# W_out's slabs turned on VectorE in 32 x 32 squares instead of on TensorE, with norm_w applied to the attention heads

## The chip, the cores and the metric

The kernel runs on one core of a Trainium2 chip (trn2). The metric is the device time of the whole launch in microseconds, the median of three runs. All data are float32.

## The reference, cut to what matters

The whole computation is a block of five stages on x of shape (4, 512, 512): a recurrent mix (bi-directional WKV), a gated-delta attention with 16 query heads and 32 value heads, a residual, a second WKV mix and a binarised linear layer. The change touches only the end of the attention: each value head's output h is normalised, multiplied by `norm_w` (one weight for each of the 128 head dimensions) and by silu(z), and then projected with `W_out`.

```python
h = core.astype(jnp.float32)                     # (4, 512, 32, 128)
h = h * jax.lax.rsqrt(jnp.mean(h * h, axis=-1, keepdims=True) + EPS)
h = norm_w * h * jax.nn.silu(z.astype(jnp.float32))
out = jnp.einsum('bsf,df->bsd', h.reshape(Bq, Sq, HV * HD), W_out)   # W_out: (512, 4096)
...
x = x + _L0_attn_ref(...)
```

For one value head the projection is a product of h (512 tokens x 128) with the transpose of a slab of `W_out`, 512 x 128. TensorE contracts over the partitions, so it needs the slab with its 128 head dimensions f on the partitions and the 512 outputs d along the row. In memory `W_out` has d as rows: the slab must be turned.

## The kernel before, in words

**Units and steps.** The attention's work is cut into 64 units, numbered n = b * 16 + hq: batch b (0 to 3) and query head hq (0 to 15); a unit has two value heads, h = 0 and 1. The loop at the end of the kernel (line 1706) makes 66 steps. A step i works on several units at once, each at a different stage: unit i + 6 (K in the plan, keys), i (F, projections and queries), i - 1 (C, the chunks of the recurrence), i - 2 (O, the output's norm, W_out's slab) and i - 3 (W, the output product). The table `plan` (line 1173) lists, for each of 22 slots of a step, what is issued in which order; slots count from 0. Every instruction goes through `InOrder` (line 72), so each engine executes exactly in this written order. SP issues almost all DMAs, in the same order, and a DMA that waits for its buffer or its data holds all later DMAs on SP.

**W_out's slab in batch 0.** Only the first batch reads W_out itself. `out_start(n, h)` (line 451) loads the 512 x 128 slab of head h in slots 13 (h = 0) and 15 (h = 1), with d on the partitions, as four blocks of 128, into a buffer of the pool `ld` with tag "raw" (four buffers of 2 KB per partition, shared with all other slab loads). `out_turn(n, h)` (line 471) turns it with four TensorE transposes into one PSUM bank, in slots 18 and 19. `out_end` (line 478) copies the bank to SBUF on ScalarE and multiplies by norm_w (`nw`, one scalar per partition) on the way: for h = 0 in two halves, the right half into a "raw" buffer of its own, `b12`; for h = 1 in one piece. The tile `wo` has seven slots of 256 columns. `out_forms` (line 492, slot 20) makes the four sums T1 to T4 of a Strassen-Winograd product from the four quarters B11, B12, B21, B22; `spare` puts it on VectorE for every fourth unit and on GpSimd otherwise. T3 and T4, T1, T2 take the other slots of `wo`. Last, SP stores `wo` and `b12` in the DRAM scratch `wosc`.

**The other batches** load `wo` from `wosc` in slot 13. The very last unit has a plain product and loads B11, B12 (index 7 of `wosc`), B21 and B22.

**The head's side.** `head_turn` (line 989) turns the normalised head output on TensorE, `head_end` (line 995, slots 7 and 10) copies the bank to `hS` on ScalarE with a plain copy, `head_forms` makes four sums, and `out_product` (line 1013) multiplies seven times. The results are added to x by VectorE in `out_add`.

**Neighbours that matter.** In batch 0 the slabs of W_qkvz are turned in the same way: `slab_start` loads, `slab_turn` transposes on TensorE, `slab_end` (line 426) copies on ScalarE, after which `project` (line 505) uses the slab. The slab of K goes through slots 3, 4 and 5, that of F's last value head through slots 9, 10 and 11. `gap_load(F + 1, "t")` in slot 21 loads the tile `dkt` for the next step; GpSimd masks it (slot 1) and ScalarE exponentiates it in slots 3 and 4, ahead of the slab copy of slot 4. `queries_end` (slot 21) multiplies dkt on VectorE with ps_kq. `inverse_load` (slot 16), `gap_load(K + 1, "d")` (slot 18) and `key_blocks` (slot 19) are SP's other DMAs around the change. `wkv_over` (slots 18, 19) holds the half reciprocals that some steps have on VectorE.

The profile has one line number for nearly everything, line 80, the helper through which all instructions pass. Groups are therefore told by tile: ps_wo is the bank of W_out's turn, woraw its load, b is b12, wo the seven slots, w a slab of W_qkvz, ps_p the bank of `project`.

Of the kernel before, what the change touches and what calls it, by code (L numbers as in the profile page):

```python
# [9 lines left out]
F32 = mybir.dt.float32  # L10
I32 = mybir.dt.int32
AF = mybir.ActivationFunctionType
ALU = mybir.AluOpType
# [3 lines left out]
P = 128  # L17
# [23 lines left out]
def kernel(  # L41
# [21 lines left out]
    B, S, D = x.shape  # L63
    HV = A_log.shape[0]
    HQ = HV // 2
    HD = norm_w.shape[0]
    KT = D // P
# [15 lines left out]
    V, A, G, T, Q = (InOrder(e) for e in (nc.vector, nc.scalar, nc.gpsimd, nc.tensor, nc.sync))  # L83
    NB = P // BS
    NM = 2 * NC
    NU = B * HQ
# [6 lines left out]
    def bank(tag, name):  # L93
        return pp.tile([P, 512], F32, tag=tag, name=name, bufs=banks[tag])


    ident = const.tile([P, P], F32, name="ident")
# [7 lines left out]
        out=tri_le, in_=tri_le, compare_op=ALU.is_ge, fill=0.0, base=0,  # L105
# [5 lines left out]
        out=tri_gt, in_=tri_gt, compare_op=ALU.is_gt, fill=0.0, base=0,  # L111
# [8 lines left out]
    for i in range(3):  # L120
        t = const.tile([P, NM, P], F32, name=f"inv_t{i}")
        G.memset(t, 0.0)
        inv_t.append(t)
        t = const.tile([P, NM // 2, 3 * BS], F32, name=f"inv_n{i}")
# [7 lines left out]
    nw = const.tile([P, 1], F32, name="nw")  # L132
# [6 lines left out]
    wosc = dram.tile([HQ, P, 8, D // 2], F32, name="wosc")  # L139
# [6 lines left out]
    with ExitStack() as main:  # L146
# [4 lines left out]
        ld = main.enter_context(tc.tile_pool(name="ld", bufs=4))  # L151
# [12 lines left out]
        def unit(n):  # L164

            return (*divmod(n, HQ), units.setdefault(n, {}))
# [32 lines left out]
        scale = const.tile([P, B], F32, name="scale")  # L199
# [240 lines left out]
        SB = {"B11": 0, "B21": 1, "B22": 2, "T1": 3, "T2": 4, "T3": 5, "T4": 6}  # L440
# [4 lines left out]
        D2 = D // 2  # L445

        def spare(i):

            return V if i % GROUP == 2 else G

        def out_start(n, h):

            b, hq, u = unit(n)
            if n == NU - 1:
                w = u[f"wo{h}"] = wp.tile([P, D], F32, **WO_LAST[h], name=f"wo_{n}_{h}")
                for i, at in enumerate(((0, 7), (1, 2))[h]):
                    Q.dma_start(out=w[:, i * D2 : (i + 1) * D2], in_=wosc[hq, :, at])
                return
            if h == 0:
                u["wo"] = wp.tile([P, 7, D2], F32, tag="wo", name=f"wo_{n}")  # L460
                if b:
                    Q.dma_start(out=u["wo"], in_=wosc[hq, :, :7])
            if b == 0:
                raw = u[f"woraw{h}"] = ld.tile([P, KT, P], F32, tag="raw", name=f"woraw_{n}_{h}")
                f = (2 * hq + h) * HD
                Q.dma_start(out=raw, in_=W_out[:, f : f + HD].rearrange("(n p) f -> p n f", p=P))


        WO_LAST = ({"tag": "wk", "bufs": 1}, {"tag": "wx", "bufs": 3})

        def out_turn(n, h):
            b, hq, u = unit(n)
            if b == 0:
                ps = u[f"wops{h}"] = bank("pj", f"ps_wo_{n}_{h}")
                for k in range(KT):
                    T.transpose(ps[:, k * P : (k + 1) * P], u[f"woraw{h}"][:, k, :], ident)

        def out_end(n, h):
            b, hq, u = unit(n)
            if b:  # L480
                return
            w, ps = u["wo"], u[f"wops{h}"]
            if h == 0:
                u["b12"] = ld.tile([P, D2], F32, tag="raw", name=f"b12_{n}")
                A.activation(w[:, 0], ps[:, :D2], AF.Copy, scale=nw)
                A.activation(u["b12"], ps[:, D2:], AF.Copy, scale=nw)
            else:
                A.activation(
                    w[:, 1:3].rearrange("p i d -> p (i d)"), ps, AF.Copy, scale=nw
                )  # L490

        def out_forms(n):
            b, hq, u = unit(n)
            if b:
                return
            w, b12, E = u["wo"], u["b12"], spare(n + 2)
            for out_, x_, y_ in (("T1", b12, "B11"), ("T2", "B22", "T1"), ("T3", "B22", b12), ("T4", "B21", "T2")):
                x_, y_ = (w[:, SB[v]] if isinstance(v, str) else v for v in (x_, y_))
                E.tensor_tensor(w[:, SB[out_]], x_, y_, ALU.subtract)
            if B > 1:  # L500
                Q.dma_start(out=wosc[hq, :, :7], in_=w)
                Q.dma_start(out=wosc[hq, :, 7], in_=b12)


        def project(n, r, half, tag="pp"):
# [489 lines left out]
        def head_end(n, h):  # L995
            b, hq, u = unit(n)
            if h == 0:
                u["hS"] = u1p.tile([P, 7, S // 2], F32, tag="hT", name=f"hS_{n}")

            at = u["hS"][:, 0:4:3] if h == 0 else u["hS"][:, 1:3]  # L1000
            A.copy(at, u["ps_h"].rearrange("p (t s) -> p t s", t=2))

        def head_forms(n):
            if n == NU - 1:
# [159 lines left out]
        def last_add(b, c):  # L1164
# [7 lines left out]
        K, F, C, O, W = AHEAD, 0, -1, -2, -3  # L1172
# [60 lines left out]
             (turn_end, F, 3), (square, F, 0), (key_matrix, K, 1), ("wkv", wkv_over, 0),  # L1233
             (gap_load, K + 1, "d"), (slab_start, K + 1, 1), ("sub", 17, None)],

            [(z_product, C, 1, 0), (out_turn, O, 1), (out_end, O, 0), (key_blocks, K), ("wkv", wkv_over, 1), ("gate", gates_rows), ("sub", 18, None)],

            [(chunk_t, C, 3), (norms, F, 0), (queries, F), (z_silu, C, 0), (out_end, O, 1),
             (out_forms, O), ("wkv", wkv_end), ("sub", 19, None)],

            [(z_product, C, 1, 1), (chunk_t_end, C, 3), (norms_copy, F, 0), (queries_end, F, 0), (queries_end, F, 1),
# [528 lines left out]
```

## Time and profile before

| | |
|---|---|
| median of three runs | 3054.6 us (3053.82 to 3056.66) |
| the profiled execution | 3053.92 us, its span 3052.2 us |
| mean granted TensorE clock | 0.985 |
| W_out's turn on TensorE | 128 matmuls of 128x128, 239.9 to 945.6 us |
| W_out's copies on ScalarE | 16 of 128x512, 32 of 128x256; 473 to 689 ns each |
| copies of the heads, hS<-ps_h | 128 of 128x512, 581 ns each |
| loads of W_out, woraw | 32 DMAs of 256 KB, 3.3 us to landing |
| stores wosc<-wo, wosc<-b | 16 of 896 KB, 3.7 us; 16 of 128 KB, 4.4 us |
| DMA packets | 422465, 351.75 MB, mean 115 GB/s |

How to read it: TensorE has two rows, PE for matmuls and transposes and PEld for the loading of the stationary operand, which overlaps. DVE is VectorE, ACT ScalarE, POOL GpSimd, SP the queue that issues DMAs. Batch 0's share of the span is about 240 to 960 us; one step takes some 44 to 49 us there.

### The profile page before, as it was taken

Reading aid. Unit: us, or ns where it says so; the run is one execution under the profiler, and the core shown is the slowest. Engines: PE = TensorE matmul, PEld = TensorE weight load, DVE = VectorE, ACT = ScalarE, POOL = GpSimd, SP = SyncE. Lnnn points to the kernel's source line nnn. Section 1 sums busy time; section 2 is a strip of 40 time slices with the busy share of each in tenths; the row PEclk is TensorE's granted clock in tenths of the full one; section 3 lists DMA queues with packets and bytes.
Section 4 is the critical chain, followed back from the end, with each engine's and each line's share of the span. In section 5 each row is a group of like instructions: output and inputs, shape, how many; then the busy total and the mean of one; then the engine's idle time right before and its main releaser. Section 6 shows DMA issues by size and latency. Waiting matters only on the chain.

```text
span 3052.2 us, 60274 instructions
## 1 busy us (share of the span) xinstructions
PE 2945.0 (96%) x20816; PEld 2124.5 (70%) x20816; DVE 2285.3 (75%) x5101; ACT 1881.6 (62%) x5145; POOL 1475.2 (48%) x3249
## 2 busy tenths in 40 slices
PE   7679999999999999999999999999999999999998
PEld 4447677777777677677777776777777677776765
DVE  7858777778767887788766887778876767687654
ACT  3566666666666666666666666666666566656552
POOL 3126463574634556265543646266443525365313
PEclk9789999999999999999999999999999999999999
DMA  5325454454453433234334433333433333433322
GB/s 135 96 83 164 126 152 134 137 167 123 138 164 113 141 94 117 82 92 131 100 105 121 123 94 107 98 117 102 117 107 110 112 97 92 118 107 108 123 81 82
DMA packets 422465, 351.75 MB, mean 115 GB/s; under 512 B 219857, under 2 KB 337617, under 8 KB 421777
## 3 DMA queue, kind: packets, MB, share of 16 engines
q1 hardware_dynamic: 420240, 347.27, 38.4%
q8 instruction: 167, 2.74, 0.4%
q14 instruction: 138, 1.12, 0.1%
q10 hardware_dynamic: 1920, 0.62, 0.1%
HBM read 268.87 MB, written 78.91 MB: 114 GB/s over the span
## 4 chain that ended last, share of the span: by engine, by line
PE 75%; DVE 10%; POOL 5%; ACT 5%; DMA 2%; issue 2%; SPq 0%; POOLq 0%; ACTq 0%; DVEq 0%
PE ps_p L80 23%; PE ps_z L80 12%; PE ps_out L80 11%; PE ps_w L80 4%; PE ps_s L80 4%; DVE y L80 3%; PE ps_o L80 3%; PE ps_st L80 2%; PE ps_j L80 2%; PE ps_kq L80 2%; PE ps_f L80 2%; POOL t L80 2%; POOL L L80 2%; PE ps_v L80 1%; PE ps_i L80 1%
## 5 line engine op out<-in xcount | busy, mean ns | idle before, releaser
L80 PE MATMUL ps_p<-cT,w 128*128 128x512 f32 x2000 | 958.2, 608 | 16.0 <-ACT w L80 13.6
L80 DVE SCALAR_TENSOR_TENSOR y<-ps_p,cw,y 128x511 f32<-128x511 f32 (+2 forms) x768 | 572.3, 746 | 267.2 <-ACT y L80 252.7
L80 PEld LDWEIGHTS ps_p<-cT,w 128*128 128x128 f32 x2000 | 358.5, 193 | 318.3 <-issue 271.9
L80 PE MATMUL ps_z<-w,cT 128*128 128x256 f32 x2048 | 479.1, 381 | 5.1 <-ACT w L80 5.1
L80 PE MATMUL ps_out<-wo,hS 128*128 128x256 f32 (+1 forms) x1780 | 459.7, 392 | 18.1 <-DVE sums L80 10.3
L80 PEld LDWEIGHTS ps_z<-w,cT 128*128 128x128 f32 x2048 | 376.4, 192 | 48.0 <-ACT w L80 5.3
L80 PEld LDWEIGHTS ps_out<-wo,hS 128*128 128x128 f32 x1780 | 312.9, 191 | 65.8 <-issue 10.4
L80 ACT ACT_TABLE_LOAD x153 | 196.3, 1283 | 174.1 <-DVE y L80 151.4
L80 DVE TENSOR_TENSOR x<-x,ps_out 128x512 f32<-128x512 f32 x240 | 163.7, 685 | 145.2 <-PE ps_out L80 145.2
L80 POOL TENSOR_TENSOR rs_t_k<-rs_y_k 128x4 f32<-128x4 f32 x171 | 57.8, 338 | 441.0 <-DVE rs_y_k L80 432.5
L80 POOL TENSOR_TENSOR L<-L,t 128x30 f32<-128x30 f32 (+14 forms) x450 | 246.6, 548 | 34.8
L80 POOL TENSOR_TENSOR t<-L 128x30 f32<-128x30 f32 (+14 forms) x450 | 229.1, 509 | 31.5 <-DMA L<-blocks_m 0.8
L80 DVE SCALAR_TENSOR_TENSOR o<-o,rs_y_o,nz 128x128 f32<-128x128 f32 x512 | 200.1, 451 | 14.2 <-POOL rs_y_o L80 13.9
L80 ACT ACTIVATE y<-ps_p,cw 128x512 f32<-128x512 f32 x256 | 174.0, 680 | 53.3 <-PE ps_p L80 53.1
L80 ACT ACTIVATE junk<-o 128x128 f32<-128x128 f32 x512 | 157.8, 308 | 75.7 <-DVE o L80 66.9
L80 ACT ACTIVATE v<-y 128x512 f32<-128x512 f32 x128 | 80.7, 630 | 198.4 <-DVE y L80 198.3
L80 ACT ACTIVATE qs<-ps_s,eg 128x128 f32<-128x128 f32 x384 | 119.9, 363 | 133.7 <-DVE r L80 109.2
L80 ACT ACTIVATE dkt<-dkt,gsum 128x128 f32<-128x128 f32 x512 | 162.6, 392 | 50.0 <-POOL dkt L80 49.7
L80 ACT ACTIVATE wd<-ps_w,eg 128x128 f32<-128x128 f32 x384 | 118.5, 361 | 82.7 <-PE ps_w L80 82.4
L80 ACT ACTIVATE dkd<-dkd,gsum 128x128 f32<-128x128 f32 x512 | 156.4, 388 | 17.2 <-POOL dkd L80 16.5
L80 PEld LDWEIGHTS ps_o<-w,dkt 128*128 128x128 f32 x1024 | 153.8, 192 | 14.4 <-ACT w L80 2.1
L80 POOL TENSOR_TENSOR rs_t_o<-rs_y_o 128x8 f32<-128x8 f32 x192 | 38.6, 201 | 256.9 <-DVE rs_y_o L80 232.8
(295 smaller groups left out, 5846.9 us busy)
## 6 DMA issues: line engine op xcount, KB each, us to landing
w<-wsc SPq DMA_DIRECT2D x288, 256.0 KB, 5.1
wo<-wosc SPq DMA_DIRECT2D x47, 896.0 KB, 4.9
dkd<-gsc SPq DMA_DIRECT2D x64, 512.0 KB, 4.1
dkt<-gsc SPq DMA_DIRECT2D x64, 512.0 KB, 4.9
wraw<-in_L_attn_W_qkvz_dram SPq DMA_DIRECT2D x96, 256.0 KB, 3.0
wsc<-w SPq DMA_DIRECT2D x90, 256.0 KB, 2.1
wosc<-wo SPq DMA_DIRECT2D x16, 896.0 KB, 3.7
blocks_m<-dkd SPq DMA_DIRECT2D x256, 32.0 KB, 1.8
```

Of the source, the lines that this page charges most:

```text
L80: return lambda *args, **kw: tc.keep_in_program_order(op(*args, **kw))
```

## The change

W_out's slab is loaded differently: the 128 columns f of the slab are cut into four strips of 32, the 512 rows d into 16 strips of 32. Each of four DMAs brings one strip of f onto its own 32 partitions; partition a * 32 + i then holds W_out[m * 32 + i, f + a * 32 + j] at column m * 32 + j. A square of 32 x 32 thus lies already where it belongs, and only has to be turned inside itself. VectorE's transpose turns every 32 x 32 square in its place, from SBUF to SBUF: two instructions of 128x256 for h = 0 (in slot 18, straight into the slots B11 and T3 of `wo`) and one of 128x512 for h = 1 (in slot 19). The runs in DRAM and in SBUF become 128 bytes instead of 512.

TensorE's transposes, their PSUM banks, ScalarE's three copies and the tile b12 are gone. B12 waits in T3's slot until T3 overwrites it. It is stored in `wosc` only for the one unit of batch 0 whose head the very last unit shares (n = 15), ahead of the forms. norm_w is now applied on the head's side, in `head_end`: the plain copies of all 64 units become activations with a scale per partition.

```diff
             if b == 0:
-                raw = u[f"woraw{h}"] = ld.tile([P, KT, P], F32, tag="raw", name=f"woraw_{n}_{h}")
+                raw = u[f"woraw{h}"] = ld.tile([P, D], F32, tag="raw", name=f"woraw_{n}_{h}")
                 f = (2 * hq + h) * HD
-                Q.dma_start(out=raw, in_=W_out[:, f : f + HD].rearrange("(n p) f -> p n f", p=P))
+                for a in range(4):
+                    Q.dma_start(
+                        out=raw[a * 32 : (a + 1) * 32].rearrange("i (m j) -> i m j", j=32),
+                        in_=W_out[:, f + a * 32 : f + (a + 1) * 32].rearrange(
+                            "(m i) j -> i m j", i=32
+                        ),
+                    )
...
         def out_turn(n, h):
             b, hq, u = unit(n)
-            if b == 0:
-                ps = u[f"wops{h}"] = bank("pj", f"ps_wo_{n}_{h}")
-                for k in range(KT):
-                    T.transpose(ps[:, k * P : (k + 1) * P], u[f"woraw{h}"][:, k, :], ident)
-
-        def out_end(n, h):
-            b, hq, u = unit(n)
             if b:
                 return
-            w, ps = u["wo"], u[f"wops{h}"]
+            w, raw = u["wo"], u[f"woraw{h}"]
             if h == 0:
-                u["b12"] = ld.tile([P, D2], F32, tag="raw", name=f"b12_{n}")
-                A.activation(w[:, 0], ps[:, :D2], AF.Copy, scale=nw)
-                A.activation(u["b12"], ps[:, D2:], AF.Copy, scale=nw)
+                V.transpose(out=w[:, SB["B11"]], in_=raw[:, :D2])
+                V.transpose(out=w[:, SB["T3"]], in_=raw[:, D2:])
             else:
-                A.activation(
-                    w[:, 1:3].rearrange("p i d -> p (i d)"), ps, AF.Copy, scale=nw
-                )
+                V.transpose(out=w[:, 1:3].rearrange("p i d -> p (i d)"), in_=raw)
...
-            w, b12, E = u["wo"], u["b12"], spare(n + 2)
-            for out_, x_, y_ in (("T1", b12, "B11"), ("T2", "B22", "T1"), ("T3", "B22", b12), ("T4", "B21", "T2")):
-                x_, y_ = (w[:, SB[v]] if isinstance(v, str) else v for v in (x_, y_))
-                E.tensor_tensor(w[:, SB[out_]], x_, y_, ALU.subtract)
+            w, E = u["wo"], spare(n + 2)
+            if n % HQ == (NU - 1) % HQ and B > 1:
+                Q.dma_start(out=wosc[hq, :, 7], in_=w[:, SB["T3"]])
+
+            for t, a, b in (
+                ("T1", "T3", "B11"), ("T2", "B22", "T1"), ("T3", "B22", "T3"), ("T4", "B21", "T2"),
+            ):
+                E.tensor_tensor(w[:, SB[t]], w[:, SB[a]], w[:, SB[b]], ALU.subtract)
             if B > 1:
                 Q.dma_start(out=wosc[hq, :, :7], in_=w)
-                Q.dma_start(out=wosc[hq, :, 7], in_=b12)
...
-            A.copy(at, u["ps_h"].rearrange("p (t s) -> p t s", t=2))
+            A.activation(at, u["ps_h"].rearrange("p (t s) -> p t s", t=2), AF.Copy, scale=nw)
...
-            [(z_product, C, 1, 0), (out_turn, O, 1), (out_end, O, 0), (key_blocks, K), ("wkv", wkv_over, 1), ("gate", gates_rows), ("sub", 18, None)],
-
-            [(chunk_t, C, 3), (norms, F, 0), (queries, F), (z_silu, C, 0), (out_end, O, 1),
+            [(z_product, C, 1, 0), (out_turn, O, 1), (key_blocks, K), ("wkv", wkv_over, 1), ("gate", gates_rows), ("sub", 18, None)],
+
+            [(chunk_t, C, 3), (norms, F, 0), (queries, F), (z_silu, C, 0), 
              (out_forms, O), ("wkv", wkv_end), ("sub", 19, None)],
```

## The prediction, as put on record before the result

> **What bounds the kernel now.** I first read the busy shares of the page. The columns are busy time, share of the span, instructions.
>
> ```profile
> PE 2945.0 (96%) x20816; PEld 2124.5 (70%) x20816; DVE 2285.3 (75%) x5101; ACT 1881.6 (62%) x5145; POOL 1475.2 (48%) x3249
> ```
>
> A share of 96% is an average, so I asked for the stretch in which the change works, the steps of batch 0. Columns: stretch, its length, busy of PE, PEld, DVE, ACT, POOL, clock, DMA share, GB/s.
>
> ```profile
> 240.00:960.00 720.00, 711.64 (x5293) 527.07 (x5292) 540.47 (x1198) 489.50 (x1318) 380.81 (x835) 1.00 0.47 143
> ```
>
> TensorE idles 8.4 of 720 us there, at full clock. What leaves its queue shortens the stretch, unless another engine then arrives late. What leaves the queue is seen in TensorE's timeline of one step (start, duration, first to last of a group):
>
> ```profile
> 285.70 1.89 PE L80 MATMUL ps_z<-w,cT 128*128 128x256 f32 x8
> 287.43 0.60 PE L80 MATMUL ps_wo<-ident,woraw 128*128 128x128 f32 x4
> 287.87 1.89 PE L80 MATMUL ps_z<-w,cT 128*128 128x256 f32 x8
> 289.60 0.60 PE L80 MATMUL ps_wo<-ident,woraw 128*128 128x128 f32 x4
> 290.03 0.61 PE L80 MATMUL ps_o<-w,dkt 128*128 128x128 f32 x4
> ```
>
> The durations overlap (0.60 us is the latency of four); the price of a group is from its start to the next start: 287.87 - 287.43 = 0.44 and 290.03 - 289.60 = 0.43 us. Neither group waits.
>
> Third, the waits of TensorE in that stretch. Its largest is the matmuls ps_p for ScalarE's w: 3.8 us in 5 times. The chain of waits shows one of them (start, length):
>
> ```profile
> 294.95 6.37 DMA dkt<-gsc
> ...
> 301.45 1.10 POOL dkt L80
> ...
> 304.58 0.48 ACT w L80
> ...
> 305.10 1.99 PE ps_p L80 x4
> ```
>
> So the stall of 1.23 us ahead of 305.10 hangs on when SP issued the load of dkt. SP's timeline says why that was 294.95:
>
> ```profile
> 289.51 1.88 SPq L80 DMA_DIRECT2D blocks_m<-dkd  x4
> 294.04 0.34 SPq L80 DMA_DIRECT2D wosc<-wo  x1
> 294.42 0.43 SPq L80 DMA_DIRECT2D wosc<-b  x1
> 294.95 0.86 SPq L80 DMA_DIRECT2D dkt<-gsc  x1
> ```
>
> After blocks_m (done 291.39) SP stands 2.65 us for the store of wo, which needs the four forms on GpSimd. GpSimd's timeline has the first of them late:
>
> ```profile
> 290.79 0.80 POOL L80 TENSOR_TENSOR wo<-b,wo 128x256 f32<-128x256 f32 x1 [3.18 <-ACT b L80]
> ```
>
> It idled 3.18 us for b, the copy that takes over the load buffer of woraw1 and hence waits for the second group of transposes. Over the stretch GpSimd waits 44.2 us for b in 12 times, and SP 21.7 us for GpSimd's wo.
>
> **Part by part.** All counts are for the 16 units of batch 0 unless said otherwise.
>
> *TensorE's transposes go.* 32 groups x 0.435 us = 13.9 us. They stand in the queue of an engine that is full, so all of it is on the path: -13.9 us.
>
> *ScalarE's copies out of PSUM go.* Per unit 0.47 + 0.47 + 0.69 us, 26 us in all. ScalarE is busy 68% of the stretch; worth nothing by itself.
>
> *VectorE gets three turns per unit*, two of 128x256 and one of 128x512. No row shows the operation. Lower bound: VectorE's fastest row of SBUF to SBUF, ek<-k at 128x512 in 0.42 us, gives 0.9 us per unit. Upper bound: reciprocal, 128x256 in 1.72 us, gives 6.9 us for 1024 columns. [...] I take 1.5 and keep 0.9 to 2.5, with 6.9 as the far end.
>
> What is queued behind them: key_matrix's second half, the half reciprocals, chunk_t_end of chunk 3, queries_end. TensorE waits for queries_end: it frees the bank of ps_kq for inverse_1 and makes dkt ready for ps_o. In the step shown queries_end finishes at 293.41 and ps_o starts at 296.37: 2.96 us of cover. VectorE also idles 0.80 us for ps_kq ahead of queries_end, which takes up the first of the delay. Since TensorE gets there 0.87 us sooner (two groups), 2.96 + 0.80 - 0.87 = 2.9 us of extra VectorE time are hidden. 1.5 and 2.5 are both under that: 0 us. Where VectorE makes the forms (each fourth unit) it stood 3.88 us for b, which goes, so more is hidden.
>
> *Forms and the load of dkt.* The turns wait for no TensorE work, only for their loads. key_matrix ends at 286.86 in this step; with two turns of 0.42 and a half reciprocal of 1.7 us the last turn runs at about 289.4 and ends at 290.1, where ScalarE's wo copy ended at 291.8. Three forms of 0.73 us follow it: 292.3, not 294.02. SP, which arrives later because of the loads (next part), is at the store of wo near 292.3 to 293.3. The store of b (0.53 us with its gap) is gone, so dkt is issued at 292.8 to 293.8 instead of 294.95. Its transfer, queued behind 128 KB less, lands sooner by another 0.4 us (128 packets of 1 KB at 46 ns over 16 engines, the medians of the trace's packet records). ScalarE's w is then 1.6 to 2.5 us earlier while TensorE arrives 0.87 us earlier: of the stall of 1.23 us at most 0.5 stays in this step, which has the most loads, and none in the others. I count 3.4 of the 3.8 us: -3.4 us. If the loads cost SP more than I think, the stall stays, and this is the first rival.
>
> *The loads of W_out*: one DMA of 512 packets of 512 B per half becomes four DMAs, together 2048 packets of 128 B. [...] Issue: the near row is blocks_m, four in 1.9 us, so SP spends 1.4 us more per half. The first half is issued in slot 13, after which SP mostly stands for slab_end(C, 4) anyway (from 615.00 to 619.22 in one step): hidden, but for the step shown, which stores a group as well and has only 0.3 us of it, 1.1 us late. The second half is directly ahead of the store of slab 5, which it delays by some 0.8 us, and with it inverse_load, gap_load and key_blocks; both are in the 292.3 to 293.3 above. inverse_load is read by inverse_1 13 us later. [...] 0 us, with up to 1 us per unit, 16 us, at the bad end. In batch 0's last unit, the form T3 must wait once for its own store, some 4.4 us on GpSimd: under 1 us on the path.
>
> *The norm_w scale moves to hS*: 128 copies turn from COPY (0.581 us) into ACTIVATE with a scale per partition. The near row of this shape, y<-ps_p,cw, is 0.680 us: +0.10 us each, 12.8 us of ScalarE. In batches 1 to 3 ScalarE is busy 63% and no ps_p waits for a slab copy: 0. In batch 0 one of the two stands in slot 10 directly ahead of slab_end(F, 3), for which project(F, 3) waits about 0.18 us in every step (psn to ps_p: 0.54 us where 0.35 is the work). ScalarE has run without a gap there since the silu, so 16 x 0.10 = +1.6 us. The last head's pair at the end of the kernel: +0.2 us. The other end is 0, if the gap moves.
>
> *Load buffers*: without b the next slab's load no longer waits for b's store to land; its cover was already enough. 0.
>
> **Sum.** The profiled execution took 3053.9 us (span 3052.2). -13.9 - 3.4 + 1.6 + 0.2 = -15.5, which makes 3038.4. It ran 0.7 us under the median of 3054.6, so the forecast is 3039.1 us.
>
> **Rivals.**
> *1. Only TensorE's share is gained.* SP's issues cost more (0.55 us as in inverse_load, and the queue pushes back, as in the one woraw issue of 1.49 us), so dkt is no earlier and TensorE, earlier by 0.87 us, stalls in more steps. Then 3.4 us are not gained, and up to 0.3 us per step is given back, 4.8 us: 3043 to 3048. For it: SP's burst from slot 15 has no gap until the store of wo. Against: 2.65 us of standing there.
> *2. More is gained.* hS's 0.1 us is hidden and stalls of some tenths at other places go as well (all idle of the stretch is 8.4 us, 2.8 of it in the gates' step): 3034.
> *3. Slower: the turn of four-byte elements is slow.* If it takes c us per unit, everything over 2.9 lands on ps_o and inverse_1 of the next step, 16 x (c - 2.9). It eats the gain of 15.5 at c = 3.9 us, 3.8 ns per element. [...] For it: no row shows a turn, and VectorE is busy 75% already. [...]
> *4. The gain is lost in VectorE's order.* VectorE's out_add frees banks for ps_out; pushed 1 us late in each step it costs about 0.8 us x 16: 3052. For: VectorE has under 3 us idle between slots 16 and 2. Against: in batches 1 to 3 VectorE is as full (572 of 720 us) with TensorE at 709.
>
> **Chances.** Forecast (3036 to 3042) 0.50; rival 1 0.22; rival 2 0.12; rival 4 0.08; rival 3 0.08. 0.2% is 6.1 us, about what a measurement of this kernel tells from no change: under 3048.5 is faster. That gives faster 0.86, same 0.06, slower 0.08. The range leaves out rival 3 and most of rival 4: 3033 to 3047.
>
> **What would show it.** In the profile after: no ps_wo; the groups of ps_z back to back; turns of about 0.4 and 0.7 us on VectorE (over 1.3 us each: rival 3). POOL's wait for b gone, dkt's load issued 1.5 us or more earlier within the step, and TensorE's wait for w in the stretch near zero (still 3 us or more: rival 1). hS rows at 0.68 us. woraw lands before its turn; a VectorE wait for woraw of over 1 us per step would make the forecast wrong.

## The result and the profile after

The changed kernel takes 3060.0 us (median of 20 runs, 3053.4 to 3064.1) where the kernel before takes 3054.4 us (20 runs beside it, 3050.3 to 3058.1): a ratio of 1.0016, 95% interval 1.0010 to 1.0022. The prediction was 3039.1 us. The profiled execution took 3059.2 us, its span is 3057.3 us. Some 20 us are missing.

The page's busy shares, then the stretch of batch 0, with the columns as in the prediction:

```profile
PE 2942.0 (96%) x20688; PEld 2113.0 (69%) x20688; DVE 2303.3 (75%) x5149; ACT 1866.2 (61%) x5097; POOL 1475.5 (48%) x3249
```

```profile
240.00:960.00 720.00, 699.10 (x5103) 511.53 (x5102) 550.26 (x1234) 463.25 (x1261) 380.16 (x829) 1.00 0.48 137
```

128 matmuls have left TensorE, as planned, but it idles 20.9 of 720 us here, not 8.4. What took their place is in TensorE's waits from 240 to 490 us (engine and tile, what it waited for, total us, times, longest):

```profile
PE ps_x L80 <- DVE x L80: 5.7, 3, 2.2
PE ps_p L80 <- ACT w L80: 4.2, 8, 1.4
PE ps_out L80 <- DVE sums L80: 3.9, 5, 1.1
```

Before, there was only one entry in that stretch:

```profile
PE ps_p L80 <- ACT w L80: 3.2, 4, 1.2
```

Two entries are new, and both are waits for VectorE to empty a PSUM bank (one of TensorE's output buffers). To see when the time goes, I took the lengths of the steps, from the first ps_w<-vb of a step to that of the next:

| start in the trace of before | before | after |
|---|---|---|
| 246 us (step 3) | 47.3 | 50.5 |
| 294 us (4) | 48.6 | 51.0 |
| 342 us (5) | 48.3 | 49.6 |
| 391 us (6) | 47.3 | 48.8 |
| 438 us (7) | 47.4 | 49.8 |
| 539 to 949 us (9 to 17), each | 43.2 to 47.6 | up to 0.9 less, 5.1 less in all |

From step 9 to 17 most steps get shorter, as forecast, by up to 0.9 us each; the 5.1 us in all are less than nine times the 0.87 us of two groups of transposes. Steps 3 to 7 give 10.8 us back. They differ from the later ones in two ways: the keys' slab is still turned in them, and steps 3, 4, 5 and 7 carry a column block of the next batch's WKV mix, whose tiles are ps_k, ps_x and the copy k.

The order of TensorE's work is that of before, but for the transposes that left. The timeline of step 3, after the change:

```profile
251.59 0.60 PE L80 MATMUL ps_k<-ident,raw 128*128 128x128 f32 x4
252.02 0.60 PE L80 MATMUL ps_w<-ident,wraw 128*128 128x128 f32 x4
252.53 1.13 PE L80 MATMUL ps_out<-wo,hS 128*128 128x256 f32 x4
254.44 1.13 PE L80 MATMUL ps_out<-wo,hS 128*128 128x256 f32 x4 [0.78 <-DVE sums L80]
...
258.73 1.98 PE L80 MATMUL ps_p<-cT,w 128*128 128x512 f32 x4 [0.54 <-ACT w L80]
260.55 0.60 PE L80 MATMUL ps_w<-ident,wraw 128*128 128x128 f32 x4
263.27 0.66 PE L80 MATMUL ps_x<-ident,raw_x 128*128 128x128 f32 x4 [2.13 <-DVE x L80]
```

The same places in the kernel before:

```profile
251.87 2.03 PE L80 MATMUL ps_out<-wo,hS 128*128 128x256 f32 x8
...
258.13 0.60 PE L80 MATMUL ps_w<-ident,wraw 128*128 128x128 f32 x4
258.56 0.60 PE L80 MATMUL ps_x<-ident,raw_x 128*128 128x128 f32 x4
```

There the two ps_out stand as one group of eight without a gap, and ps_x follows ps_w after 0.43 us. Here the second ps_out waits for VectorE to copy out the first, and ps_x waits for the copy of an earlier ps_out. That is what it looks like when two neighbours have the same bank.

SP's timeline at the end of one step holds the other half of the matter:

```profile
287.42 2.56 SPq L80 DMA_DIRECT2D woraw<-in_L_attn_W_out_dram  x4
290.08 0.52 SPq L80 DMA_DIRECT2D wsc<-w  x1
290.64 2.31 SPq L80 DMA_DIRECT2D inv_t<-blocks_t  x4
293.00 2.83 SPq L80 DMA_DIRECT2D inv_n<-blocks_n  x6
295.87 0.43 SPq L80 DMA_DIRECT2D dkd<-gsc  x1
296.40 0.38 SPq L80 DMA_DIRECT2D wraw<-in_L_attn_W_qkvz_dram  x1
296.87 1.88 SPq L80 DMA_DIRECT2D blocks_m<-dkd  x4
298.86 0.38 SPq L80 DMA_DIRECT2D wosc<-wo  x1
299.34 0.39 SPq L80 DMA_DIRECT2D dkt<-gsc  x1
```

SP goes from blocks_m straight to the store of wo, as forecast; from 240 to 960 us it stands 3.9 us for GpSimd's wo, before 21.7. But it arrives later. The step starts at 297.47, so dkd is issued 1.6 us ahead of it and dkt 1.9 us into it. In the kernel before, that step starts at 293.65:

```profile
288.50 0.43 SPq L80 DMA_DIRECT2D dkd<-gsc  x1
```

So dkd was 5.2 us ahead there, and dkt (294.95) 1.3 us into it.

### The profile page after: what moved, and what is told of

Its sections match the earlier page's. It is cut to its first block, busy times and chain, and to the rows that moved or that the text cites. A ratio compares the mean times of both kernels' runs of the same rounds, so it can differ in the third digit from the quotient of the medians.

```text
span 3057.3 us, 60072 instructions
## 1 busy us (share of the span) xinstructions
PE 2942.0 (96%) x20688; PEld 2113.0 (69%) x20688; DVE 2303.3 (75%) x5149; ACT 1866.2 (61%) x5097; POOL 1475.5 (48%) x3249
## 4 chain that ended last, share of the span: by engine, by line
PE 72%; DVE 11%; POOL 6%; ACT 5%; issue 3%; DMA 2%; SPq 0%; POOLq 0%; ACTq 0%; DVEq 0%
PE ps_p L80 23%; PE ps_z L80 11%; PE ps_out L80 11%; PE ps_w L80 4%; PE ps_s L80 4%; DVE y L80 4%; PE ps_o L80 3%; PE ps_st L80 2%; PE ps_j L80 2%; POOL L L80 2%; POOL t L80 2%; PE ps_f L80 2%; PE ps_kq L80 2%; DVE o L80 1%; PE ps_i L80 1%
## 5 line engine op out<-in xcount | busy, mean ns | idle before, releaser
L80 PE MATMUL ps_p<-cT,w 128*128 128x512 f32 x2000 | 963.7, 610 | 15.3 <-ACT w L80 14.1
L80 PE MATMUL ps_out<-wo,hS 128*128 128x256 f32 (+1 forms) x1780 | 460.7, 392 | 22.8 <-DVE sums L80 14.8
L80 ACT ACTIVATE dkd<-dkd,gsum 128x128 f32<-128x128 f32 x512 | 156.4, 388 | 49.6 <-POOL dkd L80 49.1
L80 PEld LDWEIGHTS ps_o<-w,dkt 128*128 128x128 f32 x1024 | 155.6, 192 | 15.6 <-ACT w L80 2.1
```

The source lines that it names most:

```text
L80: return lambda *args, **kw: tc.keep_in_program_order(op(*args, **kw))
```

## The experiments

Fourteen kernels ran. The table gives each one's ratio to runs of the kernel before on the same chip and, as a common scale, the ratio's distance from 1 times 3054.4 us (where a difference between two kernels is given below, it is taken from this column). Each interval is 2 to 5 us wide to either side, and small differences mean little. Each kernel has one traced execution, from which its steps and waits are read; those of e5 and e10 are the slowest of four and of five. The last two columns count, among the four WKV steps 3, 4, 5 and 7, those in which ps_out 4 has the bank of ps_out 3, and those in which ps_x has the bank of ps_out 5, read from the built program. TensorE's order puts these tiles next to each other or nearly so.

| kernel | W_out's loads per half | ratio (95%) | us | ps_out 4 | ps_x |
|---|---|---|---|---|---|
| after | four, 128 B | 1.0016 (1.0010 to 1.0022) | +4.9 | 4 | 4 |
| e1 mask of dkd first | four, 128 B | 1.0054 (1.0039 to 1.0069) | +16.5 | 4 | 4 |
| e2 as e1 | one, 512 B | 0.9971 (0.9960 to 0.9982) | -8.9 | 0 | 0 |
| e3 as e1 | four, 512 B | 0.9988 (0.9981 to 0.9995) | -3.7 | 1 | 0 |
| e4 as e1 | one, 128 B | 0.9979 (0.9971 to 0.9988) | -6.4 | 0 | 0 |
| e5 dkd early | four, 128 B | 0.9949 (0.9932 to 0.9965) | -15.6 | 0 | 4 |
| e6 old load | one, 512 B | 0.9957 (0.9942 to 0.9971) | -13.1 | 0 | 0 |
| e7 before, new loads | four, 128 B | 1.0015 (1.0008 to 1.0022) | +4.6 | 0 | 0 |
| e8 before, dkd early | one, 512 B | 0.9953 (0.9938 to 0.9968) | -14.4 | 0 | 0 |
| e9 after, e6's banks | four, 128 B | 0.9996 (0.9988 to 1.0004) | -1.2 | 0 | 0 |
| e10 e6, after's banks | one, 512 B | 1.0033 (1.0021 to 1.0045) | +10.1 | 4 | 4 |
| e11 e9, dkd early | four, 128 B | 0.9922 (0.9908 to 0.9936) | -23.8 | 0 | 0 |
| e12 before, norm_w on hS | one, 512 B | 0.9999 (0.9991 to 1.0007) | -0.3 | 0 | 0 |
| e13 e8, before's banks | one, 512 B | 0.9950 (0.9938 to 0.9963) | -15.3 | 0 | 0 |
| e14 e11, old load | one, 512 B | 0.9901 (0.9886 to 0.9916) | -30.2 | 0 | 0 |

### First round: the order on GpSimd, the number of DMAs, the packets

In the trace of after, GpSimd runs the reciprocal root of the head norm ahead of the mask of dkd; in before it was the other way round (step 4: the mask at 293.97 us and the root from 295.37 in before, the root from 299.32 and the mask at 302.59 in after). Both plans have the root first, so here the kernel before departs from its plan. It is thus not so that every engine runs exactly in the written order, as the description of the kernel before has it: on GpSimd the build decides too. e1 puts the mask first; e2 to e4 keep that and change the load, so W_out's squares lie in other places than the product wants.

```diff
# e1, all four
-            [(chunk_w, C, 0), (out_product, W, 0), (z_silu, O, 1), (chunk_w_end, C, 0),
-             (out_norm, O), (out_root, O), (gap_mask, K, "d"), ("load",)],
+            [(chunk_w, C, 0), (out_product, W, 0), (gap_mask, K, "d"), (z_silu, O, 1), (chunk_w_end, C, 0),
+             (out_norm, O), (out_root, O), ("load",)],
# e2: one DMA, 512 packets of 512 B
+                Q.dma_start(out=raw.rearrange("p (n j) -> p n j", j=P),
+                    in_=W_out[:, f : f + HD].rearrange("(n p) j -> p n j", p=P))
# e3: four DMAs of 128 packets of 512 B
+                for a in range(KT):
+                    Q.dma_start(
+                        out=raw[:, a * P : (a + 1) * P], in_=W_out[a * P : (a + 1) * P, f : f + HD])
# e4: one DMA of 2048 packets of 128 B
+                Q.dma_start(out=raw.rearrange("p (m j) -> p m j", j=32),
+                    in_=W_out[:P].rearrange("p (m k) -> p m k", k=2 * HD)[
+                        :, :, h * HD + 32 * (hq % 4) : h * HD + 32 * (hq % 4) + 32])
```

> The changed kernel with one call moved: gap_mask(K, d) stands ahead of z_silu in slot 0, so GpSimd masks dkd before the root of the output norm, as it did in the kernel before; all other engines keep the order of the changed kernel. Theory A (SP: the six more DMA issues per unit keep SP busy some 4 us longer in each step and push the loads of dkd and dkt): nothing is gained, within 5 us of the changed kernel's 3060, since dkd isn't there earlier. Theory B (the planner's new order on GpSimd, root first and mask second, makes ScalarE late): the loss goes, about 3043. Theory C (VectorE's 1.6 us of turns per unit delay what is behind them): 3058 to 3062. Theory D (128-byte packets): 3058 to 3062.

Measured 3070.6 us, 12 us more than after. Here, with both kinds of bad neighbours in place, the other order on GpSimd makes good nothing of the loss. With the mask ahead, a late dkd holds the root too, and VectorE's out_scale behind the root: from 240 to 490 us VectorE waits 4.5 us in 4 times for the root, in after never.

> e1 with the kernel-before's load of W_out: one DMA of 512 packets of 512 B per head instead of four DMAs with 2048 packets of 128 B. The blocks then lie in the old layout, so what VectorE turns isn't W_out's transpose; all instructions on all other engines are those of e1. A: gains what the prediction had, 3038 to 3045. B: as e1, both about 3043. C: no gain against the changed kernel, 3058 to 3062. D: 3038 to 3045.

Measured 3046.0 us. With the old load the gain is mostly there, although VectorE's turns and the scale at hS are in this kernel. They cannot carry the loss.

> e1 with four DMAs per head that bring 128 packets of 512 B each (one block of 128 rows of W_out per DMA): the issues of the changed kernel, the packets of the kernel before. The layout is the old one, so what is turned isn't W_out's transpose. A: as slow as e1 (3056 to 3062). B: as e1. C: 3058 to 3062. D: as e2, 3038 to 3045.

Measured 3052.3 us, 5 us more than e2 with four issues in place of one. The two intervals just meet, and e3 has one bad neighbour where e2 has none, so not all of it need be the issues.

> e1 with one DMA per head that brings 2048 packets of 128 B: the packets of the changed kernel with a single issue. It reads other places of W_out (128 rows, a run of 128 B every 1 KB), so the product isn't the reference's. A: as e2, 3038 to 3045. B: as e1. C: 3058 to 3062. D: as slow as e1, 3056 to 3062.

Measured 3048.1 us, 2.5 us more than e2 with the small packets. That is within the two intervals. The puzzle is the sum: 5 and 2.5 us apart, but 25 us together (e1 against e2). Between the two traced executions it is 31.5 us, 21 of them in the steps 3 to 7.

### Second round: is it dkd?

dkd's lead over the step shrinks with the loads. The medians of the steps 3 to 7 are 5.2 us in before, 4.5 in e2, 2.9 in e3, 3.1 in e4, 2.5 in e1 and 2.8 in after. My theory was that it is then late. e5 moves its load out of the way, e6 is the change with the old load and nothing else, e7 and e8 are the matching halves on the kernel before.

```diff
# e5 (on after) and e8 (on before)
-             (turn_end, F, 3), (square, F, 0), (key_matrix, K, 1), ("wkv", wkv_over, 0),
-             (gap_load, K + 1, "d"), (slab_start, K + 1, 1), ("sub", 17, None)],
+             (turn_end, F, 3), (square, F, 0), (key_matrix, K, 1), ("wkv", wkv_over, 0),
+             (slab_start, K + 1, 1), ("sub", 17, None)],
-            [(project, F, 0, 0), (turn, F, 2), (tap, F, 3, 0), (taps, F, 3), ("store",), ...
+            [(project, F, 0, 0), (turn, F, 2), (tap, F, 3, 0), (taps, F, 3), (gap_load, K + 1, "d"), ("store",), ...
```

> The changed kernel with one line of the plan moved: the load of dkd for unit K+1 stands in slot 13, ahead of both loads of W_out, instead of slot 18, behind them. TensorE's, VectorE's and ScalarE's orders stay as they are; on GpSimd the mask of dkd comes earlier. Theory 'dkd': the eight DMAs per step hold SP some 2 us longer, dkd is issued only 1.6 us ahead of the next step (5.2 us before the change), its mask and exponent are late, ScalarE's copy of k stands behind the exponent and VectorE's gates behind that. Then this kernel loses nothing to it: dkd issued over 10 us ahead of the step, steps 3 to 7 at 46 to 47.5 us instead of 48.8 to 51, 3041 to 3047 us. Theory 'traffic': the 2048 small packets per half slow the other transfers, or dkt (still behind them) is what is late: 3055 to 3062 us, steps 3 to 7 stay at 49 to 51.

The total came out as the theory wanted, 3042.1 us, but the steps 3 to 7 did not: in the traced execution they took 51.4, 52.3, 48.4, 46.4 and 50.8 us, no better than in after. These lengths are not quite comparable, because this execution took 3048.4 us and TensorE had a lower granted clock in it (0.97, 0.93 and 0.97 in the steps 3, 4 and 7; the last section comes back to this). What stands against the theory as the whole account is a wait: from 240 to 490 us ps_x waits 5.9 us for VectorE's x, as in after (5.7). Part of the gain is elsewhere, in the step at 196 us (2.9 us) and in the steps with the gates.

> The kernel before with the load of dkd moved to slot 13, as in e5: the control. Theory 'dkd': before the change dkd had its lead of 5.2 us already, so an earlier load is worth little: 3051 to 3055 us. If the place of this load is worth as much here as in the changed kernel (10 us or more: 3045 us or less), then e5's gain does not come from the change's loads being made up for.

3041.4 us: the early load is worth 14.4 us to the kernel before. In e5 it brought 20.5 us against after, so most of e5's gain is not the change's loss made good; some 6 us of it may be. A total that agrees is no proof; the control and the waits had to be looked at.

> The changed kernel with W_out loaded as before the change, one DMA of 512 packets of 512 B per half, GpSimd's order as the planner gives it; the squares then lie in the wrong places, so this is the change without the cost of its loads. Theory 'dkd' and theory 'traffic' agree here: nothing is lost, and the sum of the prediction stands but for norm_w: 3038 to 3044 us. If it is 3050 or more, the loss is not in the loads, and the turns or the scale at hS carry it.

3042.5 us, 13.1 us under before: the change without its loads gives most of the 15.5 us that were summed. Steps 3 to 7 take 46.1 to 47.0 us. The loss is in the loads, or in something that comes with them.

> The kernel before, with TensorE's transposes and ScalarE's copies kept, and only the loads of W_out made as in the change: four DMAs of 512 packets of 128 B per half (the data lies in other places than the transposes want, so W_out's part of the result is not the reference's). Theory 'dkd': dkd has 5.2 us of lead over the step in the kernel before and loses about 2 to 2.5 us of it, which leaves 2.7 to 3.2, as in the runs with one half of the load's change: 0.5 to 1 us in each of steps 3 to 7, 3057 to 3061 us. If the loads' cost adds to any kernel alike, the difference of the runs before (24.6 us) shows here as well: about 3079 us. If the loads are innocent: 3054 us.

3059.8 us, +4.6 us: on the kernel before, the same eight DMAs cost a quarter of what they cost in the changed one (18 us, after against e6).

### What the programs showed

e1 and e3 differ in nothing but the shape of four DMAs, and no engine's order of work differs but for one mask on GpSimd. I compared which semaphores TensorE's instructions wait for in the two programs as built: in e1 ps_x waits for VectorE, in e3 it waits for nothing. (In the traces ps_x waits 7.0 us in 4 times in e1 from 240 to 490 us, in e3 never.) The tag "pj" has three PSUM banks, and the build decides which of them a tile gets. For step 3 it had chosen (tile and bank, in TensorE's order):

```
before  ps_k:0 ps_w:2 ps_out_3:1 ps_out_4:0 ps_out_5:1 ps_w:2 ps_x:0
after   ps_k:2 ps_w:1 ps_out_3:0 ps_out_4:0 ps_out_5:2 ps_w:0 ps_x:2
e6      ps_k:2 ps_w:1 ps_out_3:0 ps_out_4:2 ps_out_5:0 ps_w:2 ps_x:1
```

In before and in e6, ps_out_4 takes ps_k's bank, which ScalarE's copy k frees. In after it takes the bank of ps_out_3, the tile just ahead of it, and ps_x takes that of ps_out_5. The next round writes the two choices out as lists, one digit for each tile of the tag: 776 of 1206 digits differ between after and e6.

### Third round: the banks

In e9 to e11 the banks of "pj" are given by hand: three tags of one bank each, and a list of digits that says which one the next tile takes.

```diff
+    PJ = iter("0210210210210210210212012012020...")
     def bank(tag, name):
+        if tag == "pj":
+            return pp.tile([P, 512], F32, tag="pj" + next(PJ), name=name, bufs=1)
         return pp.tile([P, 512], F32, tag=tag, name=name, bufs=banks[tag])
```

> The reverse: e6 (one DMA of 512 B packets per half, squares in the wrong places) with the banks of the changed kernel given by hand. Theory 'banks': 3048 to 3057 us, ps_out waits for sums by about 1 us and ps_x for x by about 2 us in the steps 3, 4, 5 and 7. Theory 'SP': as e6, 3039 to 3045 us, since the loads are the old ones.

3061.6 us, 23 us more than e6 with the same loads, orders and instructions: the banks alone do that. The two largest of TensorE's waits from 240 to 490 us in e10:

```profile
PE ps_out L80 <- DVE sums L80: 8.8, 4, 3.2
PE ps_x L80 <- DVE x L80: 6.3, 4, 1.7
```

The two waits of after are back, with the loads of before. The expected 3048 to 3057 was too small; part of what lies above it is the granted clock, which is 0.94 in step 3 and 0.97 in step 7 here and 1.00 in e6 (last section).

> The changed kernel, with the three PSUM banks of the tag pj given by hand, in the order in which they came out in e6 (the change with the old loads). In the changed kernel as built, ps_out 3 and ps_out 4 follow each other in one bank in five of the steps 3 to 9, and ps_x stands in the bank of ps_out 5; in e6 they don't. Theory 'banks': the loss is TensorE's wait for VectorE's copy out of a bank that it has just filled, and what follows from that; the loads themselves cost the 2 to 6 us that e3, e4 and e7 show. Then 3043 to 3049 us, steps 3 to 7 at 46.5 to 48.5, no wait of ps_x for x. Theory 'SP' (dkd and dkt late behind the eight DMAs): 3056 to 3062 us, steps as in the changed kernel, since no load is moved.

3052.8 us: better than after, which has the same loads and the same order on every engine, by 6.1 us, but not the 3043 to 3049 of the theory of banks alone. TensorE's waits in the same stretch of e9:

```profile
PE ps_out L80 <- ACT k L80: 7.5, 4, 2.5
PE ps_p L80 <- ACT w L80: 2.9, 7, 1.6
```

Both waits for VectorE are gone and another has come: ps_out_4, now in ps_k's bank, waits for ScalarE's copy k. ScalarE's timeline in step 4, where TensorE waits 2.48 us, says why that is late:

```profile
297.68 1.28 ACT L80 ACT_TABLE_LOAD   x1 [1.01 <-DMA dkd<-gsc]
300.70 2.44 ACT L80 ACTIVATE dkd<-dkd,gsum 128x128 f32<-128x128 f32 x8 [1.74 <-POOL dkd L80]
303.05 0.56 ACT L80 COPY k<-ps_k 128x512 f32<-128x512 f32 x1
```

The copy stands behind the exponent of dkd, which waits for GpSimd's mask. The mask in turn waits for more than the load. GpSimd's timeline of the same step, with the first and the last instruction of the root:

```profile
296.29 0.20 POOL L80 TENSOR_TENSOR rs_t_o<-rs_y_o 128x8 f32<-128x8 f32 x1 [2.64 <-DVE rs_y_o L80]
...
299.41 0.20 POOL L80 TENSOR_TENSOR rs_y_o<-rs_y_o,rs_t_o 128x8 f32<-128x8 f32 x1
299.57 1.09 POOL L80 TENSOR_SCALAR_AFFINE_SELECT dkd<-dkd 128x1024 f32<-128x1024 f32 x1
```

dkd landed at 297.6; its mask starts 2 us later, behind the twelve instructions of the root, which began 1.85 us into the step. The starts, in us from the start of the step (in step 6 there is no copy k):

| | e6 | e9 | e1 | e11 |
|---|---|---|---|---|
| W_out's loads per half | one, 512 B | four, 128 B | four, 128 B | four, 128 B |
| dkd's mask | ahead of the root | behind it | ahead of it | ahead, load early |
| dkd landed, steps 3, 4, 5, 7 | 0.3, -0.4, 0.7, 0.0 | 2.5, 3.2, 1.6, 0.6 | 2.6, 3.0, 1.5, 0.5 | over 5 ahead |
| copy k starts | 5.2, 5.9, 5.9, 5.2 | 7.3, 8.6, 8.6, 7.3 | 6.5, 6.7, 5.9, 5.2 | 5.2, 6.0, 5.9, 5.2 |

So two things make the copy k late in e9. The load lands later, which alone (e1) delays the copy in the steps 3 and 4 only. And the build put the mask behind the root, in e9 as in after, which delays it in all four: of 9.6 us between e9 and e6, some 7.5 are this order, as far as e1 with its other banks can stand for the loads alone. e9 and e6 therefore differ in the loads and in GpSimd's order, and no run has the new loads, e6's banks and the mask ahead. In after the late copy shows less, because ps_out_4 does not use ps_k's bank there: it waits for ps_out_3's instead.

> The changed kernel with the banks of e9 and the early load of dkd of e5. Theory 'banks': e5 kept its loss in the steps 3 to 7 because its banks were bad as well (ps_x waits for x there), and gained at other places what e8 gains; so the gains add: 3028 to 3036 us, under every kernel so far. If e5 kept its loss because dkt is late (issued 1.7 and 2.9 us into the step there), this one keeps it too: 3039 to 3045 us.

3026.5 us, with the change's own loads: neither the banks nor the late copy k hold TensorE any more. The early load does two things at once, since the mask too now runs ahead of the root, 5.2 us before the step. This version beats every other one that computes the whole result, by 0.8% against before (0.9922, 0.9908 to 0.9936). The only entry over 0.2 us among TensorE's waits in the stretch:

```profile
PE ps_p L80 <- ACT w L80: 4.7, 8, 2.5
```

The longest of these eight, 2.5 us, is in the step at 289 us (51.0 us long), where dkt is issued 2.6 us into the step. Beside e5, which has the same loads in the same places and the same order on every engine, this is 8.2 us for the banks alone: in e5's build ps_x stands behind ps_out 5 in all four WKV steps.

> The kernel before with norm_w moved to the copy of the turned output alone; W_out's copies out of PSUM are plain. The prediction's term: +1.8 us (0.10 us in each of 16 steps, and the end), 3056 to 3058 us. If the gap ahead of project(F, 3) moves: no difference. 5 us or more would say that this part carries the loss.

3053.4 us; the interval spans -2.7 to +2.1 us. The forecast of +1.8 us is inside it, and so is nothing. A size below what this measurement resolves; a loss of 5 us is excluded. The run is not quite the term by itself: the plain copies of W_out's banks are some 0.1 us shorter each than those with a scale (587 instead of 688 ns for 128x512).

### Fourth round: what the early load is worth by itself

> The kernel before with the early load of dkd of e8, and with the banks of the kernel before given by hand, so that only the place of the load is changed. If e8's gain of 14 us comes from the load: 3038 to 3044 us. If it came from other banks (195 of 1174 tiles had another bank in e8): 3052 to 3056 us.

3040.6 us: with the banks held, the gain of e8 stays. It is the load's. Steps 3 to 7 are 47.9, 48.5, 48.3, 46.7 and 47.9 us, as in before: dkd is not late there in the kernel before, and the gain lies at the step at 196 us (2.5 us) and behind 949 us (10 us). In e9 against e11, the same move brings 22.6 us. The 7 us beyond e13's 15.3 are an estimate, from these two differences, of what the late copy k costs the changed kernel, by the load and by GpSimd's order together. The traces agree: in the steps 3 to 17 the move takes 7.2 us off e9 and 0.1 us off before.

> e11 with the old load of W_out, one DMA of 512 B packets per half (squares in the wrong places): what the change could give if its loads cost nothing at all. If the loads of the change cost time only through dkd and the banks: as e11, 3023 to 3029 us. If the eight DMAs still cost by dkt, as the one step of 51.0 us in e11 (289 to 341 us) suggests: 4 us or more under e11, 3018 to 3023 us.

3025.8 us, a ratio of 0.9901 where e11 has 0.9922. By the ratios the loads of W_out still cost some 6 us in e11, as the second theory has it; by the time itself the run falls into the range of the first, and the two intervals overlap, so this is not settled. Between the traced executions there are 5.3 us, most of them in that one step, 51.0 us against 46.4, and from 240 to 490 us TensorE waits 1.0 us for w in place of 4.7: this speaks for dkt. Against e13, which ran beside it, the change without the cost of its loads brings 14.8 us (the two have different banks). The prediction's sum was 15.5.

## Why the prediction was wrong, step by step

*TensorE's transposes go: -13.9 us.* Right. Wherever nothing else interferes (steps 15 to 17) a step is 0.8 to 0.9 us shorter, two groups of 0.435 us.

*ScalarE's copies: 0.* No run speaks against it and none has it alone. The 26 us of copies are gone; that ScalarE's busy time in the stretch fell by just as much, although hS takes some 3 us more, is chance, since the stretch cuts the steps at other places.

*VectorE's turns: 1.5 us per unit, hidden.* Right. The forecast took its 1.5 us from VectorE's plain copies, two of 0.42 us and one of 0.69. Their rows in before:

```profile
L80 DVE COPY o<-ps_o 128x256 f32<-128x256 f32 x64 | 26.6, 416 | 0.1
...
L80 DVE COPY sums<-ps_out 128x512 f32<-128x512 f32 x12 | 8.2, 686 | 1.6 <-PE ps_out L80 1.6
```

The rows of after, for the two shapes:

```profile
L80 DVE STREAM_TRANSPOSE wo<-woraw 128x256 f32<-128x256 f32 x32 | 12.2, 420 | 0.0
...
L80 DVE STREAM_TRANSPOSE wo<-woraw 128x512 f32<-128x512 f32 x16 | 10.9, 680 | 0.0
```

Two of 0.42 and one of 0.68 are 1.52 us; the rows of the plain copies were the right neighbours. No run shows the 2.5 us that the prediction kept as its high end. VectorE never waits for woraw: it idles ahead of none of the 48 turns. That the turns are hidden is shown by e6, which has them and the forecast's gain nearly whole.

*Forms and the load of dkt: -3.4 us.* The cause was read rightly, and the gain is there without the new loads. TensorE's waits for the slab w in the first third of a step were 3.45 us in the stretch before, in four steps; in e6, where dkt is issued 0.3 us ahead of step 4 as forecast, they are 0.65 us in two, and in after 3.2 us in three. GpSimd's wait for b is gone (it now waits 36.9 us for VectorE's turns, in e6 as well, at no loss), and the forms hold SP no longer. But in after SP's own issues take their place: dkt is issued 0.1 to 1.9 us into the steps 3 to 7, before 0.5 to 1.3.

*The loads of W_out: 0, with up to 16 us at the bad end.* **This is the step that failed.** The form of the loads costs 18 us, after against e6. The price of an issue was nearly right: the median of 128 is 0.49 us where 0.47 was taken from blocks_m, with a tail to 2.46 us. What was wrong is what was hidden. The prediction put the first half behind a wait of SP and booked 0.8 us for the second. In the trace a group of four DMAs takes 2.56 us (2.24 by the median) in place of one of 0.45, and dkd, next behind the groups, is issued 3.6 us later within step 4, and 2.4 us later by the medians of the steps 3 to 7. The prediction followed this delay only to dkt and to inverse_load. It says that gap_load is delayed too, and does not ask who waits for that tile: GpSimd's mask, ScalarE's exponent, the copy k behind it on ScalarE, and the bank that the copy frees. dkd's lead of 5.2 us was cover that the prediction did not name. The 1 us per unit behind the bad end of 16 us is shown by no run. It was the author's estimate for another case, a woraw that lands late, which did not happen: a load lands 2.8 us after its issue by the median in after, 3.3 in before, and VectorE waits for none. That the 16 us cover much of the 18 is luck. The packets of 128 B take 13 ns by the median of the packet records in before and after, those of 512 B 27, and DMA's share of the stretch went from 0.47 to 0.48.

*What no step of it contained:* what the build makes of the loads. The prediction took it that what isn't touched keeps its memory and its order. Which bank a tile gets is decided when the program is built, and a change of nothing but the shape of a load moved 776 of 1206 tiles, and on GpSimd the mask of dkd behind the root. The shares depend on the order in which one counts. From e6, e6's banks kept, the loads and GpSimd's order bring 12 us (e9), and after's banks then 6 us more (after). From e6, the banks alone bring 23 us (e10), and then the loads with GpSimd's order take 5 us off again. So it can't be said which is the larger part in after: TensorE waits either for VectorE or for the copy k, and each seems to hide part of the other. What the loads cost where neither comes in, or hardly, is small: 4.6 us in the kernel before (e7, with the mask ahead in the steps 3 to 9), some 6 us and unsettled between e14 and e11. The rest of e9's 12 us would then be GpSimd's order, some 6 us, which is an estimate by difference.

*norm_w on hS: +1.6 us.* The size of the operation was right (669 to 724 ns, 0.68 us forecast), TensorE's wait ahead of project(F, 3) grew from 0.11 to 0.20 us per step, and the total can't be told from none (e12).

*The rivals.* The first, that SP's issues cost more, named the place and the push-back of the queue, but priced it at 3043 to 3048 us, by dkt alone. The fourth, waits for VectorE's out_add, is what the waits of after look like; its reason, a VectorE that runs later, is not it: in e9 VectorE has the same work in the same order, and the waits are gone.

Open is by what reckoning the build chooses a bank or GpSimd's order. That it reacts to a load's shape is shown; that it does so by its own estimate of when each bank comes free fits (ps_k's bank is avoided just where dkd, and with it the copy k, comes late), but no run shows it.

## What to carry to other kernels

When a DMA is split, follow every later DMA of that queue to its readers, with the lead that each has over its first use: a tile with 5 us of lead is not safe if the queue gets 2 us longer in each half and the reader comes 0.9 us sooner. Compare the memory places of the two built programs, and each engine's order in the traces, before any theory: a wait between two neighbours of one tag may come from a bank that moved, and a late tile from an instruction that now stands ahead of its reader, in code that the change never touched. When a tile is late, look when its load landed. And judge an experiment by the waits that made the loss, and by a control, not by its total: e5's total fitted a theory that explains some 6 of its 20 us.

## What was not expected of the hardware

In e5 a wait of TensorE cost more than its length. It waited 2.63 us for w, and then:

```profile
308.25 3.78 PE L80 MATMUL ps_p<-cT,w 128*128 128x512 f32 x4 [2.63 <-ACT w L80]
311.83 1.06 PE L80 MATMUL ps_w<-ident,wraw 128*128 128x128 f32 x4
312.68 1.06 PE L80 MATMUL ps_x<-ident,raw_x 128*128 128x128 f32 x4
313.53 0.90 PE L80 MATMUL ps_w<-r,inv_t 128*128 128x128 f32 x4
314.27 1.88 PE L80 MATMUL ps_p<-cT,w 128*128 128x512 f32 x4
```

ps_p takes 3.78 us at first and 1.88 us six microseconds later; ps_x takes 1.06 instead of the 0.60 of before. The windows give the granted clock around it (the number ahead of the DMA share):

```profile
304.00:308.00 4.00, 1.63 (x52) 1.13 (x45) 3.83 (x13) 2.24 (x9) 1.09 (x1) 0.91 0.02 6
308.00:312.00 4.00, 3.75 (x5) 1.58 (x6) 1.48 (x4) 1.88 (x7) 0.00 (x0) 0.50 0.17 66
312.00:316.00 4.00, 4.00 (x18) 3.00 (x17) 0.00 (x0) 1.53 (x5) 0.00 (x0) 0.73 0.00 0
```

From the groups' starts, ps_p, ps_w, ps_x and ps_w take 6.0 us, where in the kernel before (256.35 to 259.45) the same four take 3.1: the wait cost some 3 us on top of itself. The length of the wait does not decide this by itself. In the same trace a wait of 2.15 us that ended at 259.5 was followed by a clock of 0.63 (first line); in e9 one of 2.49 us that ended at 354.3 was followed by 1.00 (second line):

```profile
260.00:264.00 4.00, 4.00 (x14) 2.44 (x13) 0.00 (x0) 2.67 (x7) 0.69 (x1) 0.63 0.11 42
...
354.00:358.00 4.00, 3.74 (x61) 3.11 (x62) 1.58 (x6) 3.66 (x14) 0.37 (x1) 1.00 0.09 32
```

After the one of 2.13 us in step 3 of after the clock was 1.00 as well (264 to 268 us). One of 2.48 us in e9, a step before the other, was followed by a longer ps_s (1.06 us at 305.07, where the same one takes 0.59 in after), and one of only 1.41 us in after, which ended at 310.42 behind one of 1.05 that ended at 305.26, by a clock of 0.58 from 310 to 314 us; ps_p takes 3.60 us there. So no length parts the two outcomes in these traces. The steps with such stalls cost more than the list of waits shows: the granted clock is 0.97, 0.93 and 0.97 in the steps 3, 4 and 7 of e5, 0.94 and 0.97 in the steps 3 and 7 of e10, which have stalls of 3.20 and 2.55 us, and 0.97 in step 4 of after.
